# A graph network with top-p attention on one Trainium2 core: the second attention's first look moved to ScalarE, its search cut into eight steps woven over three row tiles

## The chip, the cores and the metric

The program runs on one core of a Trainium2 chip. The metric is the device time of one launch in microseconds, the median of five runs. A separate profiled execution gives the trace from which all durations below are read.

## The reference, cut to what matters

There are 3327 nodes with 256 features, a sparse weighted adjacency matrix (about 1% of the entries and the diagonal), and four layers, each followed by a residual and a normalisation over the features. The change concerns the last layer alone:

```python
def _top_p_attention(X, W1, W2, W3):
    logits = (X @ W1.T @ W2.T) @ (X @ W3.T).T
    probs = softmax(logits)                      # 3327 x 3327
    # a row keeps its largest entries until their sum reaches 0.9
    keep_sorted = cumsum(sorted) - sorted < 0.9
    A = probs * mask
    return A / A.sum(-1)
R = (S + eye) / row sums                         # S is the adjacency matrix
for n in range(2):
    A = _top_p_attention(Xa, W1, W2, W3)
    Xf = R @ Xf                                  # "diffusion"
    Xa = A @ Xa                                  # "attended values"
    Z = Z + Xf @ U1[n].T + Xa @ U2[n].T
h = layernorm(X + Z)
```

The attention is computed twice, each time over the whole graph. The second attention needs the first one's output of every row.

## The kernel before

Rows are padded to 3328 and cut into 26 row tiles of 128. A row tile of either attention passes through the following parts, which the code writes as Python generators, so that a loop can lay instructions of different tiles beside each other with `next`.

- **Logits** (`scores`, lines 698 to 709): eight matmuls of 128x416 in four pairs (line 707, tile `sc`, two PSUM buffers), each copied out by ScalarE into `e`, 128x3328 (line 708). `e` has three buffers.
- **Search** for the threshold. The first attention uses `search_short`. The second uses `search_long`, since its rows keep more entries:
  - `m8` (line 813), the largest of the first 416 logits, gives a shift; ScalarE takes exp of half of it (line 817, sum `root`) and exp (line 818, sum `tot`).
  - The first look: a guess `c1` from these sums (lines 822 to 824). ScalarE counts the entries over it with Sign (line 827) while VectorE sums them with a full-width pass (line 829, sum `m1`).
  - The second look: a better guess `c2` and its negative `nc2` (lines 830 to 846). ScalarE takes Relu (line 847) and then Sign (line 848) of the whole tile.
  - From these, `k2`, `m2` and the last guess `c3` (lines 861 to 870), 128x1 operations on VectorE in a chain. Line 873 writes `z`, the entries under `c3`, a full-width pass. Then come 26 `max` of 128 columns (line 759, `cand`), six rounds of `max` and `match_replace` over 208 candidates (lines 768 and 770), the crossing of 0.9 (lines 777 to 780), the ties (lines 881 to 892, two `match_replace` of 128x1664), and the full-width pass of line 893 that zeroes all of `e` below the threshold.
- **Attended values** (`attended`): seven groups of four 128x128 transposes on TensorE (line 747, tile `tp`), copied out by ScalarE (line 749, `wt`), and 26 matmuls of 128x256 against `G` (line 751; the trace shows two passes for each matmul).
- **Diffusion** (`diffused`, `aggregated`): 26 matmuls of 128x256 with adjacency blocks that SP's queue loads in four pieces (lines 717 and 719; three buffers), and a combination on VectorE (line 737, `xf`) with a term that GpSimd prepares (lines 728 and 732). Diffusions run up to four tiles ahead.
- **Epilogue** (`second`, lines 931 to 953): VectorE joins values and diffusion (line 934, `h`), two normalisations with statistics on VectorE (lines 83 and 84, called at each) and the power -0.5 on GpSimd (lines 507 and 508), a last scaling on ScalarE (line 950) and the store.

The loop of both attentions is one (line 984): logits of a tile, one diffusion, the three steps of the search for three neighbouring tiles, then values and epilogue. A scheduler of the language then fixes the order on each engine when the program is built, from its own costs and from the order in the source. Each engine works through its list in that order, so an instruction that waits holds up all behind it on its engine. The build can be listed engine by engine without running it.

Of the kernel before, what the change touches and what calls it, by code (L numbers as in the profile page):

```python
# [18 lines left out]
P = 128  # L19
# [9 lines left out]
DA = 64  # L29
# [4 lines left out]
RP0, RPT = 6, 6  # L34
# [3 lines left out]
DL = 4  # L38
# [4 lines left out]
def gnn_kernel(ctx: ExitStack, tc: tile.TileContext, n: int, a: dict, out: bass.AP):  # L43
# [88 lines left out]
    with tc.tile_pool(name="l1b", bufs=1) as wpool, tc.tile_pool(name="l1at", bufs=2) as l1at:  # L132
# [29 lines left out]
        with tc.tile_pool(name="l1aw", bufs=1) as cwork, tc.tile_pool(name="l1c", bufs=2) as ch, \  # L162
# [318 lines left out]
    with tc.tile_pool(name="l3", bufs=1) as pool, tc.tile_pool(name="l3d", bufs=1, space=DRAM) as dram:  # L481
# [258 lines left out]
        def attended(work, psum, e, rhs):  # L740

            acc = psum.tile([P, D], F32, name="acc")
            for j0 in range(0, nt, 4):
                m = min(4, nt - j0)
                pt = psum.tile([P, 4, P], F32, name="tp")
                for j in range(m):
                    nc.tensor.transpose(pt[:, j, :], e[:, (j0 + j) * P:(j0 + j + 1) * P], ident)  # L747
                wt = work.tile([P, 4, P], F32, name="wt", bufs=3)
                nc.scalar.copy(wt[:, :m, :], pt[:, :m, :])  # L749
                for j in range(m):  # L750
                    nc.tensor.matmul(acc, wt[:, j, :], rhs[:, j0 + j, :],  # L751
                                     start=(j0 + j == 0), stop=(j0 + j == nt - 1))
            return acc

        def segment_tops(work, z):

            cand = work.tile([P, nseg * 8], F32, name="cand")
            for s in range(nseg):
                nc.vector.max(cand[:, s * 8:(s + 1) * 8], z[:, s * SEG:(s + 1) * SEG])  # L759
            return cand  # L760

        def ranked(work, cand, rounds):

            top = work.tile([P, 8 * rounds], F32, name="top")
            rest = work.tile([P, nseg * 8], F32, name="rest", bufs=1)
            for r in range(rounds):
                left = rest if r else cand
                nc.vector.max(top[:, r * 8:(r + 1) * 8], left)  # L768
                if r + 1 < rounds:
                    nc.vector.match_replace(rest, top[:, r * 8:(r + 1) * 8], left, NEG)  # L770
            return top
# [19 lines left out]
        def search_short(work, sm, e, total, v, kept):  # L791


            top = ranked(work, segment_tops(work, e), RP0)
            neg = t1(sm, "neg")
            nc.vector.tensor_scalar_mul(neg, top[:, 0:1], -1.0)
            nc.scalar.activation(e, e, AF.Exp, bias=neg, accum_out=total)
            nc.scalar.activation(top, top, AF.Exp, bias=neg)
            crossing(work, v, top, 0.0, limit(sm, total))
            nc.vector.scalar_tensor_tensor(e, e, v, e, op0=ALU.is_ge, op1=ALU.mult, accum_out=kept)  # L800
            yield

        def search_long(work, sm, e, total, v, kept):
# [5 lines left out]
            def t(name):  # L809
                return t1(sm, name)  # L810
# [12 lines left out]
            nc.vector.tensor_mul(c1, c1, total)  # L823
            nc.vector.scalar_tensor_tensor(c1, c1, 0.301, c1, op0=ALU.mult, op1=ALU.mult)

            sg, k1, m1 = t("sg"), t("k1"), t("m1")
            nc.scalar.activation(junk, e, AF.Sign, bias=c1, scale=-1.0, accum_out=sg)  # L827
            z = work.tile([P, npad], F32, name="z", bufs=1)
            nc.vector.scalar_tensor_tensor(z, e, c1, e, op0=ALU.is_ge, op1=ALU.mult, accum_out=m1)  # L829
            nc.vector.tensor_scalar(k1, sg, -0.5, npad / 2, op0=ALU.mult, op1=ALU.add)  # L830
            rc, na = t("rc"), t("na")
            nc.vector.reciprocal(rc, c1)
            nc.vector.tensor_scalar(na, m1, lim, rc, op0=ALU.subtract, op1=ALU.mult)
# [7 lines left out]
            nc.vector.reciprocal(q, q)  # L841
            c2 = t("c2")
            nc.vector.scalar_tensor_tensor(c2, p, c1, q, op0=ALU.mult, op1=ALU.mult)

            nc2, f2, k2, m2 = t("nc2"), t("fs2"), t("k2"), t("m2")
            nc.vector.tensor_scalar_mul(nc2, c2, -1.0)
            nc.scalar.activation(junk, e, AF.Relu, bias=nc2, accum_out=f2)
            nc.scalar.activation(junk, e, AF.Sign, bias=c2, scale=-1.0, accum_out=sg)  # L848

            big = t("big")  # L850
# [22 lines left out]
            nc.vector.scalar_tensor_tensor(z, e, c3, e, op0=ALU.is_lt, op1=ALU.mult, accum_out=rest)  # L873
            nc.vector.tensor_sub(base, total, rest)
            nc.vector.scalar_tensor_tensor(base, big, 1.0, base, op0=ALU.is_lt, op1=ALU.mult)
            cand = segment_tops(work, z)
            top = ranked(work, cand, RPT)
            cs = crossing(work, v, top, base, lim)

            r, up = t("r"), t("up")  # L880
            nc.vector.tensor_sub(cs, cs, top)
# [49 lines left out]
        def second(work, psum, it, acc, f, xf):  # L931

            h = work.tile([P, D], F32, name="h")
            nc.vector.scalar_tensor_tensor(h, acc, f, xf, op0=ALU.mult, op1=ALU.add)
            yield
            xb = work.tile([P, D], F32, name="t")
            nc.gpsimd.tensor_tensor(xb, X[:, it, :], b3, op=ALU.add)
            mv = small.tile([P, 2], F32, name="mv")
            stats(mv, h)
            rs = small.tile([P, 1], F32, name="rs")  # L940
            power(rs, mv)
            nc.vector.scalar_tensor_tensor(h, h, mv[:, 0:1], g3, op0=ALU.subtract, op1=ALU.mult)
            nc.vector.scalar_tensor_tensor(h, h, rs, xb, op0=ALU.mult, op1=ALU.add)
            mv = small.tile([P, 2], F32, name="mv")
            stats(mv, h)
            rs = small.tile([P, 1], F32, name="rs")
            power(rs, mv)
            nb = small.tile([P, 1], F32, name="nb")
            nc.vector.scalar_tensor_tensor(nb, mv[:, 0:1], -1.0, rs, op0=ALU.mult, op1=ALU.mult)
            nc.scalar.activation(h, h, AF.Identity, scale=rs, bias=nb)  # L950
            m = min(P, n - it * P)
            nc.sync.dma_start(out[it * P:it * P + m, :], h[:m, :])
            yield
# [29 lines left out]
        with tc.tile_pool(name="l3w", bufs=2) as work, tc.tile_pool(name="l3s", bufs=4) as sm, \  # L983
                tc.tile_pool(name="l3at", bufs=3) as atp, tc.tile_pool(name="l3p", bufs=2, space=PSUM) as psum:


            for p, search, step, lead in ((0, search_short, first, (1,)), (1, search_long, second, (2, 1, 0))):
                es, searches, xfs, todo = {}, {}, [], None
                for i in range(-lead[0], nt):
                    t = i + lead[0]  # L990
                    parts = []
                    if t < nt:
                        q = work.tile([2 * DA, P], F32, name="q")
                        nc.sync.dma_start(q, qd[p][t])
                        es[t] = work.tile([P, npad], F32, name="e", bufs=3)
                        searches[t] = search(work, sm, es[t], *(x[p][:, t:t + 1] for x in (tots, vs, kepts)))
                        parts.append(scores(work, psum, p, q, es[t]))
                    more = range(len(xfs), min(nt, i + DL + 1))
                    for j in more[:1]:
                        parts.append(diffused(work, atp, psum, p, j, xfs))  # L1000
                    if p:
                        for x in parts:
                            both(x)
                    else:
                        both(*parts)
                    if todo is not None:
                        next(todo)
                    for part in lead:
                        if 0 <= i + part < nt:
                            next(searches[i + part])  # L1010
                    for j in more[1:]:
                        both(diffused(work, atp, psum, p, j, xfs))
                    if i >= 0:
                        tot, kept = (x[p][:, i:i + 1] for x in (tots, kepts))
                        f = normalizer(sm, kept, tot)
                        todo = step(work, psum, i, attended(work, psum, es[i], G if p else X), f, xfs[i])
                        next(todo)
                next(todo)
                fl = unresolved(sm, psum, p)
                if p == 0:  # L1020
                    fl0 = fl

            fi0 = pool.tile([1, nt + 1], I32, name="fi0")
            fi1 = pool.tile([1, nt + 1], I32, name="fi1")
            nc.vector.tensor_copy(fi0, fl0)
            nc.vector.tensor_scalar_add(fl, fl, fl0[:, nt:])
            nc.vector.tensor_copy(fi1, fl)
# [45 lines left out]
        def again(p, it):  # L1073

            with tc.tile_pool(name="l3w", bufs=2) as work, tc.tile_pool(name="l3s", bufs=1) as sm, \
# [24 lines left out]
                both((second if p else first)(work, psum, it, attended(work, psum, e, G if p else X), f, xfs[0]))  # L1100

        bad = nc.values_load(fi1[0:1, nt:nt + 1])
        with tc.If(bad > 0):
# [67 lines left out]
```

## Time and profile before

| what | value |
|---|---|
| median of five runs | 4013.08 us (4001.09 to 4016.1) |
| the profiled execution's own time | 4014.39 us |
| its span, first to last instruction | 4012.6 us |
| TensorE, VectorE, ScalarE, GpSimd busy in the span | 90%, 68%, 42%, 9% |
| mean granted TensorE clock | 0.954 |
| start of the second attention's first logits (line 707) | 3052.6 us |
| first and last start of line 873 in it | 3102.4 and 3955.7 us |

The profiled execution is 1.3 us above the median. A row of a timeline or group gives line, engine, operation, written tile, read tiles, shapes, a count where equal neighbours are merged, and in brackets the idle time before it with the instruction that ended it. "Busy" columns of a window are us in which an engine worked.

### The profile page before, as it was taken

The page shows a single profiled execution, that of the slowest core. Times are in us where ns is not written, and L with a number is a line of the kernel's source. Part 1 is how long each engine was busy: PE and PEld are TensorE (multiplying, and loading weights), DVE is VectorE, ACT ScalarE, POOL GpSimd, SP SyncE. Part 2 cuts the span into 40 slices and gives each one's busy share as a digit, 9 for nine tenths or more (in the row PEclk, how much of TensorE's full clock was granted, in tenths as well). Part 3 has the DMA queues.
Part 4 walks back from the last instruction along what each step waited for, and adds up shares of the span by engine and source line. Part 5 has one row for each costly group of instructions (what it writes and reads, how often), then busy time and mean ns, then how long its engine had stood idle before and what let it go on. Part 6 is the DMA issues. An engine that isn't in the chain of part 4 may idle for free.

```text
span 4012.6 us, 41676 instructions
## 1 busy us (share of the span) xinstructions
PE 3604.4 (90%) x15071; PEld 2626.9 (65%) x15071; DVE 2723.9 (68%) x6003; ACT 1676.1 (42%) x2690; POOL 367.8 (9%) x436
## 2 busy tenths in 40 slices
PE   8999988888888877789989999999999899999985
PEld 7888754444444433378877777777777677777764
DVE  1111579999999989867743444443452999999996
ACT  0000554555554555211112333333344666666662
POOL 0000000101010101011110000000000122222210
PEclk9999999999999988899999999999999999999997
DMA  6442211111111000044422221121103222122100
GB/s 219 138 140 92 79 47 37 37 35 35 39 34 34 23 0 0 15 146 142 140 77 79 60 57 49 53 60 52 49 25 86 59 62 58 54 60 63 55 22 7
DMA packets 98960, 252.96 MB, mean 63 GB/s; under 512 B 13858, under 2 KB 48034, under 8 KB 98610
## 3 DMA queue, kind: packets, MB, share of 16 engines
q1 hardware_dynamic: 98738, 250.14, 20.4%
q8 instruction: 122, 2.00, 0.2%
q14 instruction: 100, 0.82, 0.1%
HBM read 239.88 MB, written 10.22 MB: 62 GB/s over the span
## 4 chain that ended last, share of the span: by engine, by line
PE 34%; DVE 16%; ACT 3%; issue 2%; POOL 1%; DMA 0%; SPq 0%; POOLq 0%; ACTq 0%; DVEq 0%
PE acc L751 11%; PE acc L719 7%; PE acc L649 6%; PE sc L707 3%; DVE cand L759 3%; DVE e L892 2%; DVE e L893 2%; PE tp L747 2%; PE pj L917 1%; DVE z L829 1%; DVE top L768 1%; DVE z L873 1%; DVE rest L770 1%; ACT junk L827 1%; ACT junk L848 1%
## 5 line engine op out<-in xcount | busy, mean ns | idle before, releaser
L403 DVE TENSOR_TENSOR_SCAN h<-dA,carry,db 128x512 f32<-128x512 f32 (+1 forms) x448 | 510.4, 1189 | 0.1
L459 PE MATMUL y<-h,ident 128*128 128x512 f32 (+1 forms) x896 | 443.7, 642 | 70.6 <-DVE h L406 70.2
L759 DVE MAX8 cand<-e 128x8 f32<-128x128 f32 x676 | 143.8, 279 | 497.4 <-ACT e L708 497.4
L751 PE MATMUL acc<-G,wt 128*128 128x256 f32 x1352 | 342.9, 408 | 48.4 <-ACT wt L749 48.4
L459 PEld LDWEIGHTS y<-h,ident 128*128 128x128 f32 x896 | 188.8, 218 | 288.1 <-issue 175.7
L749 ACT COPY wt<-tp 128x512 f32<-128x512 f32 (+1 forms) x364 | 186.1, 553 | 438.2 <-PE tp L747 438.0
L751 PEld LDWEIGHTS acc<-G,wt 128*128 128x128 f32 x1352 | 268.8, 204 | 120.8 <-ACT wt L749 82.2
L234 PE MATMUL cb<-F,at 128*128 128x256 f32 x1352 | 330.6, 389 | 8.3 <-ACT m L251 8.2
L708 ACT COPY e<-sc 128x416 f32<-128x416 f32 (+1 forms) x416 | 192.6, 508 | 329.4 <-PE sc L707 329.4
L751 PE MATMUL acc<-X,wt 128*128 128x256 f32 x1352 | 326.0, 386 | 3.0 <-ACT wt L749 2.8
L719 PE MATMUL acc<-X,at 128*128 128x256 f32 x1352 | 322.2, 388 | 2.5 <-issue 2.5
L234 PEld LDWEIGHTS cb<-F,at 128*128 128x128 f32 x1352 | 259.5, 195 | 88.9 <-issue 32.8
L649 PE MATMUL acc<-F,at 128*128 128x257 f32 x1352 | 310.5, 383 | 4.0 <-DVE at L646 4.0
L719 PE MATMUL acc<-F,at 128*128 128x256 f32 x1352 | 308.8, 380 | 0.0
L113 PE MATMUL acc<-xa,at 128*128 128x257 f32 x1352 | 308.2, 381 | 0.0
L719 PEld LDWEIGHTS acc<-X,at 128*128 128x128 f32 x1352 | 251.9, 192 | 76.4 <-issue 44.6
L751 PEld LDWEIGHTS acc<-X,wt 128*128 128x128 f32 x1352 | 250.3, 191 | 63.8 <-ACT wt L749 33.5
L388 ACT ACTIVATE dA<-dt,A_log 128x512 f32<-128x512 f32 (+1 forms) x448 | 281.0, 681 | 12.5 <-DVE dt L365 12.1
L707 PE MATMUL sc<-kT,q 64*128 64x416 f32 x832 | 259.8, 561 | 27.5 <-ACT e L708 26.0
L113 PEld LDWEIGHTS acc<-xa,at 128*128 128x128 f32 x1352 | 255.6, 191 | 37.4 <-issue 0.7
L719 PEld LDWEIGHTS acc<-F,at 128*128 128x128 f32 x1352 | 249.5, 189 | 46.5 <-issue 13.7
L649 PEld LDWEIGHTS acc<-F,at 128*128 128x128 f32 x1352 | 253.6, 192 | 39.1 <-DVE at L646 4.3
(297 smaller groups left out, 5362.3 us busy)
## 6 DMA issues: line engine op xcount, KB each, us to landing
at<-in_adjT SPq DMA_DIRECT2D x104, 832.0 KB, 4.5
at<-in_adjT SPq DMA_DIRECT2D x156, 448.0 KB, 3.4
at<-in_adjT SPq DMA_DIRECT2D x52, 576.0 KB, 3.7
at<-in_adjT SPq DMA_DIRECT2D x52, 320.0 KB, 3.0
at<-in_adjT SPq DMA_DIRECT2D x26, 512.0 KB, 3.5
xa<-in_x SPq DMA_DIRECT2D x1, 3328.0 KB, 13.6
xt<-in_xT SPq DMA_DIRECT2D x26, 128.0 KB, 4.1
qd<-q SPq DMA_DIRECT2D x52, 64.0 KB, 1.5
```

The source lines that it names most:

```text
L113: nc.tensor.matmul(acc, at[:, j, :], rhs[:, j0 + j, :], start=(j0 + j == 0), stop=(j0 + j == nt - 1))
L234: nc.tensor.matmul(acc, at[:, j % JC, :], X0[:, j, :], start=(j == 0), stop=(j == nt - 1))
L388: nc.scalar.activation(dA[:, g, :], dt[:, g, :], AF.Exp, scale=A[:, g, s:s + 1])
L403: nc.vector.tensor_tensor_scan(h[:, g, :], dA[:, g, :], db[g // 2][:, g % 2, :], initial=carry[:, s, g:g + 1], op0=ALU.mult, op1=ALU.add)
L459: nc.tensor.matmul(ys[g][:, :w], ident, h[:, g, :], start=False, stop=(s == DS - 1))
L649: nc.tensor.matmul(acc, at[:, j, :], F[:, j0 + j, :], start=(j0 + j == 0), stop=(j0 + j == nt - 1))
L707: nc.tensor.matmul(pl[:, :w], q[h:h + DA, :], kT[p][h:h + DA, c0:c0 + w], start=True, stop=True)
L708: nc.scalar.copy(e[:, c:c + w], pl[:, :w])
L719: nc.tensor.matmul(acc, at[:, j, :], rhs[:, j0 + j, :], start=(j0 + j == 0), stop=(j0 + j == nt - 1))
L749: nc.scalar.copy(wt[:, :m, :], pt[:, :m, :])
L751: nc.tensor.matmul(acc, wt[:, j, :], rhs[:, j0 + j, :], start=(j0 + j == 0), stop=(j0 + j == nt - 1))
L759: nc.vector.max(cand[:, s * 8:(s + 1) * 8], z[:, s * SEG:(s + 1) * SEG])
```

## The change

Everything up to the end of the first attention is left as it was. In the second attention:

- `m1` of the first look is no longer VectorE's full-width pass: ScalarE takes Relu of `e` minus `c1` (new line 837) before the Sign (839), and VectorE computes `m1 = k1 * c1 + f1` on 128x1 (842).
- `search_long` yields seven times in place of two before its end, so it has eight steps.
- `attended` yields after each group of transposes. `second` has three steps.
- The two attentions have loops of their own. That of the second weaves eight search steps of three row tiles, the seven groups of values, half logits, and single pieces of a diffusion.
- Five diffusions are made before the second row tile's logits, and there is one iteration more, since values of a tile come one iteration after its search.

New line numbers of the parts named above: `m8` 821, exps 825 and 826, `c1` 830 to 832, `nc1` 836, Relu and Sign of the first look 837 and 839, `k1` 841, `c2` and `nc2` 855 and 857, Relu and Sign of the second look 858 and 860, `k2` 873, `z` 885, tie `match_replace` 908, last pass 909, `h` 950, second scaling 959, `nb` 966.

```diff
         def search_long(...)
...
-            sg, k1, m1 = t("sg"), t("k1"), t("m1")
+            nc1, f1, sg, k1, m1 = t("nc1"), t("fs1"), t("sg"), t("k1"), t("m1")
+            nc.vector.tensor_scalar_mul(nc1, c1, -1.0)
+            nc.scalar.activation(junk, e, AF.Relu, bias=nc1, accum_out=f1)
+            yield
             nc.scalar.activation(junk, e, AF.Sign, bias=c1, scale=-1.0, accum_out=sg)
-            z = work.tile([P, npad], F32, name="z", bufs=1)
-            nc.vector.scalar_tensor_tensor(z, e, c1, e, op0=ALU.is_ge, op1=ALU.mult, accum_out=m1)
+            yield
             nc.vector.tensor_scalar(k1, sg, -0.5, npad / 2, op0=ALU.mult, op1=ALU.add)
+            nc.vector.scalar_tensor_tensor(m1, k1, c1, f1, op0=ALU.mult, op1=ALU.add)
...
             nc.scalar.activation(junk, e, AF.Relu, bias=nc2, accum_out=f2)
+            yield
             nc.scalar.activation(junk, e, AF.Sign, bias=c2, scale=-1.0, accum_out=sg)
...
-            cand = segment_tops(work, z)
+            cand = candidates(work)
+            segment_tops(cand, z, 0, nseg // 2)
+            yield
+            segment_tops(cand, z, nseg // 2)
             top = ranked(work, cand, RPT)
             cs = crossing(work, v, top, base, lim)
+            yield
...
         def second(work, psum, it, acc, f, xf):
             h = work.tile([P, D], F32, name="h")
             nc.vector.scalar_tensor_tensor(h, acc, f, xf, op0=ALU.mult, op1=ALU.add)
-            yield
             xb = work.tile([P, D], F32, name="t")
...
             power(rs, mv)
+            yield
             nc.vector.scalar_tensor_tensor(h, h, mv[:, 0:1], g3, op0=ALU.subtract, op1=ALU.mult)
...
             power(rs, mv)
+            yield
             nb = small.tile([P, 1], F32, name="nb")
...
+            es, searches, xfs = {}, {}, []
+            for i in range(-2, nt + 1):
...
+                if 0 < i:
+                    values = attended(work, psum, es[i - 1], G)
...
+                weigh(2)
+                search(i)
+                search(i + 1)
+                weigh(2)
+                search(i + 1)
+                weigh(3)
+                search(i)
+                if 0 < i:
+                    f = normalizer(sm, kepts[1][:, i - 1:i], tots[1][:, i - 1:i])
+                    result = second(work, psum, i - 1, next(values), f, xfs[i - 1])
+                next(result, None)
+                logits = start(1, i + 2, es, searches, search_long) if i + 2 < nt else iter(())
+                more = range(len(xfs), min(nt, max(i, 0) + DL + 1))
+                spread = diffused(work, atp, psum, 1, more[0], xfs) if more else iter(())
+                next(logits, None)
+                next(logits, None)
+                next(spread, None)
+                search(i + 1)
+                both(logits)
+                next(spread, None)
+                search(i + 1)
+                search(i + 2)
+                next(result, None)
+                both(spread)
+                search(i)
+                for _ in result:
+                    pass
+                for j in more[1:]:
+                    both(diffused(work, atp, psum, 1, j, xfs))
```

More of the change, by code (lines that the diff above doesn't have):

```diff
@@ L752, in attended, with last_of, segment_tops, candidates @@
                                      start=(j0 + j == 0), stop=(j0 + j == nt - 1))
[L753 to L758, printed above, removed]
+                yield None
+            yield acc
+        def last_of(steps):
+            *_, x = steps
+            return x
+        def segment_tops(cand, z, lo=0, hi=nseg):
+            for s in range(lo, hi):
                 nc.vector.max(cand[:, s * 8:(s + 1) * 8], z[:, s * SEG:(s + 1) * SEG])
-            return cand
+        def candidates(work):
+            return work.tile([P, nseg * 8], F32, name="cand")
         def ranked(work, cand, rounds):
@@ L791, in search_short @@
         def search_short(work, sm, e, total, v, kept):
-            top = ranked(work, segment_tops(work, e), RP0)
+            cand = candidates(work)
+            segment_tops(cand, e)
+            top = ranked(work, cand, RP0)
             neg = t1(sm, "neg")
@@ L875, in search_long @@
             nc.vector.scalar_tensor_tensor(base, big, 1.0, base, op0=ALU.is_lt, op1=ALU.mult)
-            cand = segment_tops(work, z)
+            cand = candidates(work)
+            segment_tops(cand, z, 0, nseg // 2)
+            yield
+            segment_tops(cand, z, nseg // 2)
             top = ranked(work, cand, RPT)
             cs = crossing(work, v, top, base, lim)
+            yield
             r, up = t("r"), t("up")
@@ L984, in gnn_kernel @@
                 tc.tile_pool(name="l3at", bufs=3) as atp, tc.tile_pool(name="l3p", bufs=2, space=PSUM) as psum:
[L987 to L1021, printed above, removed]
@@ new lines, in start @@
+            def start(p, t, es, searches, search):
+                q = work.tile([2 * DA, P], F32, name="q")
+                nc.sync.dma_start(q, qd[p][t])
+                es[t] = work.tile([P, npad], F32, name="e", bufs=3)
+                searches[t] = search(work, sm, es[t], *(x[p][:, t:t + 1] for x in (tots, vs, kepts)))
+                return scores(work, psum, p, q, es[t])
+            es, searches, xfs, todo = {}, {}, [], None
+            for i in range(-1, nt):
+                parts = []
+                if i + 1 < nt:
+                    parts.append(start(0, i + 1, es, searches, search_short))
+                more = range(len(xfs), min(nt, i + DL + 1))
+                for j in more[:1]:
+                    parts.append(diffused(work, atp, psum, 0, j, xfs))
+                both(*parts)
+                if todo is not None:
+                    next(todo)
+                if i + 1 < nt:
+                    next(searches[i + 1])
+                for j in more[1:]:
+                    both(diffused(work, atp, psum, 0, j, xfs))
+                if i >= 0:
+                    f = normalizer(sm, kepts[0][:, i:i + 1], tots[0][:, i:i + 1])
+                    todo = first(work, psum, i, last_of(attended(work, psum, es[i], X)), f, xfs[i])
+                    next(todo)
@@ new lines, in gnn_kernel, with search, weigh @@
+            next(todo)
+            fl0 = unresolved(sm, psum, 0)
+            es, searches, xfs = {}, {}, []
+            for i in range(-2, nt + 1):
+                def search(t):
+                    if 0 <= t < nt:
+                        next(searches[t])
+                values, result = iter(()), iter(())
+                if 0 < i:
+                    values = attended(work, psum, es[i - 1], G)
+                def weigh(steps):
+                    for _ in range(steps):
+                        next(values, None)
+                weigh(2)
[25 more added lines that the diff above has]
+                    pass
+                for j in more[1:]:
+                    both(diffused(work, atp, psum, 1, j, xfs))
@@ L1023, in gnn_kernel @@
+            fl = unresolved(sm, psum, 1)
             fi0 = pool.tile([1, nt + 1], I32, name="fi0")
@@ L1099, in again @@
                 both(diffused(work, atp, psum, p, it, xfs))
-                both((second if p else first)(work, psum, it, attended(work, psum, e, G if p else X), f, xfs[0]))
+                acc = last_of(attended(work, psum, e, G if p else X))
+                both((second if p else first)(work, psum, it, acc, f, xfs[0]))
         bad = nc.values_load(fi1[0:1, nt:nt + 1])
```

## The prediction

> **What bounds it now.** I read the page's totals first, then stage windows, then single rows.
>
> ```profile
> core 0: us, PE busy (x) PEld busy (x) DVE busy (x) ACT busy (x) POOL busy (x), PEclk, DMA share, GB/s
> 3049.00:3169.70 120.70, 104.67 (x450) 79.79 (x449) 78.57 (x269) 76.43 (x79) 11.46 (x17) 0.94 0.34 95
> 3169.70:3955.70 786.00, 697.37 (x3178) 538.55 (x3178) 740.94 (x2588) 517.76 (x583) 166.17 (x177) 0.95 0.18 51
> 3955.70:4012.60 56.90, 35.71 (x158) 28.93 (x156) 29.72 (x97) 8.58 (x16) 3.80 (x8) 0.80 0.02 7
> ```
>
> These windows cut the second attention by its marker, the `z` pass (line 873), once per row tile: fill until the third marker, 23 gaps, drain. A gap is 786.0 / 23 = 34.17 us. VectorE works 32.2 us of it, TensorE 30.3, ScalarE 22.5. VectorE sets the pace; TensorE is 2 us behind.
>
> The drain shows the search of one tile alone on VectorE:
>
> ```profile
> 3955.67 3.69 DVE L873 SCALAR_TENSOR_TENSOR z<-e,c 128x3328 f32<-128x3328 f32 x1
> ...
> 3964.69 0.38 DVE L768 MAX8 top<-cand 128x8 f32<-128x208 f32 x1
> ...
> 3971.94 1.87 DVE L892 MATCH_REPLACE8 e<-drop,e 128x1664 f32<-128x1664 f32 x1
> ...
> 3975.98 3.67 DVE L893 SCALAR_TENSOR_TENSOR e<-e,v 128x3328 f32<-128x3328 f32 x1
> 3979.59 0.08 DVE L893 DVE_READ_ACCUMULATOR e<-e,v 128x1 f32 x1
> ```
>
> From marker to the end of line 893: 24.0 us, less 0.4 for an `h` in it: 23.6.
>
> The fill shows the second look with nothing beside it:
>
> ```profile
> 3071.51 0.15 DVE L846 TENSOR_SCALAR nc<-c 128x1 f32<-128x1 f32 x1
> 3071.76 3.07 ACT L847 ACTIVATE junk<-e,nc 128x3328 bf16<-128x3328 f32 x1 [2.40 <-DVE s L855]
> 3074.96 3.07 ACT L848 ACTIVATE junk<-e,c 128x3328 bf16<-128x3328 f32 x1
> 3078.15 0.15 DVE L861 TENSOR_SCALAR k<-sg 128x1 f32<-128x1 f32 x1 [3.54 <-ACT junk L848]
> 3079.80 0.22 DVE L870 SCALAR_TENSOR_TENSOR c<-c,c,big 128x1 f32<-128x1 f32 x1
> ```
>
> A ScalarE pass takes 3.20 us, start to start. `nc2` to `k2` takes 6.6 us; `k2` to the next marker 1.9. **The question is what VectorE does in those 6.6 us.** In the order of the build before, all 25 gaps have `nc2` among the first `max` instructions: the two passes lie beside 26 `max`, the ranking and the ties.
>
> **The change, part by part.**
>
> *VectorE's pass leaves.* One 3.68 us pass per tile goes; `nc1` and the new `m1` add 0.15 and 0.20 (rows of lines 846 and 862). VectorE falls to 32.2 - 3.3 = 28.9 us a gap, ScalarE rises to 22.5 + 3.2 = 25.7, TensorE stays at 30.3. If no wait took its place, TensorE would set about 31.
>
> *A longer first look.* `c1` to `k1` was one ScalarE pass beside VectorE's own; it is now two, 6.4 us. In most gaps of the new order `nc1` stands near 10 us after the marker and `k1` after the ranking (4.8) and the crossing (2.4), 17.2 or later. 10 + 6.4 = 16.4: covered, cost 0. Without that cover it would be up to 6.4.
>
> *The second look is moved.* This is the costly part. I listed the new build's VectorE order and sorted the 23 gaps by where `nc2` stands: **early**, before both tie `match_replace` (6 gaps); **middle**, between them or before the last full-width pass, line 909 (5); **late**, behind line 909 (12).
>
> Late, from marker 0: 23.6 alone, 0.4 for `xf`, 0.6 for the next tile's `c1` and `nc1`, 1.0 for `k1` and its followers: line 909 ends at 25.6. The rest of the chain to `nc2` (rows of lines 839 to 846, 0.97): 26.6. Then ScalarE's list: Relu 3.2, one `wt` of 256 columns (0.37), two `sc` copies (0.92), Sign 3.2: `k2` at 34.3. Meanwhile VectorE has only `m8` and the epilogue. In seven of the twelve, `m8` stands behind `nc2` and needs an `sc` copy that stands behind Relu, so it waits until 30.7; 0.7 for it and 3.6 for the epilogue (drain, line 934 at 3998.84 to the second line 84 ending 4002.45) give 35.0. `nb`, in the middle of the `k2` chain, waits 1.26 more for GpSimd (4002.27 to 4003.53): 36.2, and 1.3 of chain: 37.5. Four of the seven also begin with the previous epilogue's second half, +1.2: 38.7. In the five others `m8` comes before: 0.7 later at `nc2`, no `wt`, 34.6 + 1.9 = 36.5. Sum: 3 x 37.5 + 4 x 38.7 + 5 x 36.5 = 449.8. Ends: 34.9 each (no copies between the passes, epilogue hidden: 26.6 + 6.4 + 1.9) and 38.9.
>
> Middle: `nc2` near 22.0, passes and copies to 29.8, the chain mixed with the epilogue to 31.7 to 33.3; 32.6, so 163.0. Early: no VectorE wait over 1 us; TensorE's 30.3 plus 0.9, a fraction of its present 3.9 idle, as its copies still queue behind ScalarE's passes: 31.2, so 187.2. Ends for these 11: 30.5 and 34.2.
>
> Gaps: 449.8 + 163.0 + 187.2 = 800.0, against 786.0: **+14.0 us**.
>
> *The fill.* The first marker comes at about 3083 instead of 3102, since the second tile's first look no longer stands ahead of it on VectorE. But five diffusions of 11.5 us now precede the second tile's logits on TensorE: 3051 + 57.5 = 3108.6, logits 6.2 (four pairs at 1.56), two exps 6.9, `c1` 0.7, first look with three `sc` copies between 8, to `nc2` 2, second look 7, chain 1.9: second marker 3141, third 31 later, 3172. Before: 3169.7. **+2.3**; between -5 and +8.
>
> *The drain.* The last tile's search has half of an epilogue inside (0.5 + 0.8): **+1.3**.
>
> *Moved at nothing:* GpSimd's powers and memsets keep their neighbours but for the next epilogue's bias sum, which may stand ahead of a power: 0.7 (row of line 732) up to 4.2 if it meets a full-width pass, inside the `nb` wait above. SP's queue issues the same loads; `at` pieces land in 3.4 us with three buffers ahead, and a TensorE gap hides them. If not, 1 us a gap.
>
> *TensorE's clock.* After a long pause TensorE is slow:
>
> ```profile
> 3979.81 1.94 PE L747 MATMUL tp<-ident,e 128*128 128x128 f32 x8 [5.26 <-DVE e L893]
> 3981.63 5.47 PE L751 MATMUL acc<-G,wt 128*128 128x256 f32 x16
> 3986.93 1.04 PE L747 MATMUL tp<-ident,e 128*128 128x128 f32 x8
> 3988.26 3.72 PE L751 MATMUL acc<-G,wt 128*128 128x256 f32 x16 [0.15 <-ACT wt L749]
> ```
>
> That is 0.9 + 1.75 = 2.65 us lost. A late gap leaves TensorE 7 us idle, so such pauses grow, but they fit in that idle time: 0 in the sum.
>
> The Trainium skill, "TensorE: Matmul & The Clock Gate", section "What's actually happening", says that an idle window of about 3.4 us halves the clock and as long a busy one restores it. An estimate by that page: 1.7 us lost per pause, 39 us if each of 23 gaps had one on the path, which would make 4070.
>
> The Trainium skill, "ScalarE: Activation LUTs", section "Step-by-step: what each stage is for", gives one element per cycle, 0.833 ns, thus 2.77 us for 3328 columns by estimate; the row says 3.20. By the page the late gaps would be 0.86 shorter, 10 us in all, making 4020.
>
> **Sum.** 4014.4 (profiled execution) + 14.0 + 2.3 + 1.3 = 4032.0; that execution stands 1.3 above the median: **4031 us**.
>
> **The rivals.** About 0.2%, 8 us, is what can be told from no change: 4005 to 4021.
>
> - *The weave works as the source is laid out* (0.20): VectorE's small operations slip between passes, so `nc2` comes out early enough and all gaps cost a middle one: 23 x 32.6 = 749.8, 36.2 less than now: 3980. For it: VectorE's 28.9 us. Against: lists are worked in order, and `nc2` is behind line 909 in 12 of 23. It decides where 6.6 us of VectorE work lie between `nc2` and `k2`.
> - *TensorE is the new bound everywhere* (0.05): 23 x 31.2 = 717.6: 3948. It needs no late gap to wait.
> - *Both sides cancel* (0.10): late gaps at 36.4: 436.8 + 163.0 + 187.2 = 787.0: about 4017.
> - *Late gaps spoil the others* (0.17): their pauses slow TensorE, transposes and `wt` copies come late, and ScalarE's passes queue behind them; early and middle gaps stay at 34.2: 449.8 + 376.2 = 826.0: 4057.
>
> **How the numbers follow.** The forecast has 0.48. Its own unknowns (late gaps at 34.9 to 38.9) reach from 4000 to 4047. The range 3975 to 4070 leaves out the TensorE-bound case and the outer ends of the first and last rivals, 0.2 together. Faster by over 0.2%: 0.25, the first two rivals; within: 0.10, the cancelling one; slower: 0.65, the forecast and the last.
>
> **What would show it.** Right: line 829's group gone, line 837 with 26 passes near 3.07 us; VectorE's share of the gaps down from 94% to about 84%; waits of `k2` (873) for Sign (860), of `m8` (821) for line 708 and of `nb` (966) for GpSimd, together 4 to 6 us per late gap; marker gaps in two groups, near 31 to 33 and 36 to 39, in the order of the list. First marker near 3083, second near 3141. Wrong: even gaps below 33, VectorE still above 90% busy, or `k2` never waiting. A row tile flagged as unresolved by the new `m1` would show as full-width passes in the repeat code and cost over 100 us (28 passes of 3.7); I see no sign of it.

## The result, and the profile after

The changed kernel takes 4021.86 us (median of 29 runs, 4016.44 to 4036.09), the kernel before 4010.56 us in the same comparisons (54 runs). The ratio is 1.003 with a 95% interval of 1.0023 to 1.0037: 9 to 15 us slower, where 18 were forecast. The profiled execution took 4022.87 us, its span is 4021.1.

The same three stages of the second attention after the change (fill, 23 gaps between markers, drain; columns as before):

```profile
core 0: us, PE busy (x) PEld busy (x) DVE busy (x) ACT busy (x) POOL busy (x), PEclk, DMA share, GB/s
3049.00:3165.40 116.40, 102.06 (x429) 76.56 (x429) 66.79 (x261) 77.53 (x80) 15.06 (x17) 0.92 0.32 92
3165.40:3961.40 796.00, 713.53 (x3187) 541.75 (x3188) 691.79 (x2593) 591.33 (x635) 99.47 (x176) 0.95 0.18 50
3961.40:4021.10 59.70, 32.72 (x146) 26.34 (x144) 29.96 (x96) 7.64 (x15) 3.74 (x8) 0.79 0.03 9
```

VectorE's work in the 23 gaps fell from 740.9 to 691.8 us, ScalarE's rose from 517.8 to 591.3, and the stage became 10 us longer, 786 to 796. Now no engine is busy for more than 90% of it. The work that left VectorE had set the pace there, and waits took its place. The waits of VectorE between 3100 and 3970 us (who waits, for whom; us in total, times, longest):

```profile
DVE k L873 <- ACT junk L860: 27.0, 8, 6.7
DVE m L821 <- ACT e L708: 24.9, 10, 3.4
DVE nb L966 <- POOL rs L508: 20.0, 23, 1.4
DVE h L959 <- POOL rs L508: 12.4, 19, 0.8
```

Before, `k2` waited 15.7 us for ScalarE in this stretch, `m8` did not appear among the waits, and `nb` waited 18.2. (The stretch is a little longer than the 23 gaps; one wait of `k2`, 6.7 us, lies in the fill.) One late gap on VectorE, from marker 3682.6 to marker 3720.2 (37.6 us), shows how the waits hang together:

```profile
3704.74 3.68 DVE L909 SCALAR_TENSOR_TENSOR e<-e,v 128x3328 f32<-128x3328 f32 x1
...
3709.18 0.15 DVE L857 TENSOR_SCALAR nc<-c 128x1 f32<-128x1 f32 x1
...
3713.22 0.59 DVE L821 MAX8 m<-e 128x8 f32<-128x416 f32 x1 [3.43 <-ACT e L708]
...
3716.46 0.48 DVE L959 SCALAR_TENSOR_TENSOR h<-h,rs,t 128x256 f32<-128x256 f32 x1 [0.77 <-POOL rs L508]
...
3717.53 0.12 DVE L873 TENSOR_SCALAR k<-sg 128x1 f32<-128x1 f32 x1
...
3718.68 0.16 DVE L966 SCALAR_TENSOR_TENSOR nb<-mv,rs 128x1 f32<-128x1 f32 x1 [0.77 <-POOL rs L508]
...
3720.21 3.69 DVE L885 SCALAR_TENSOR_TENSOR z<-e,c 128x3328 f32<-128x3328 f32 x1
```

`nc2` comes after the full-width pass of line 909, so the tile's whole search is done before the next tile's second look begins. From `nc2` to the marker pass 11 us, in which VectorE has `m8`, the epilogue and a chain of 128x1 operations, and stands still for 3.43 us because the copy that `m8` needs is behind Relu on ScalarE:

```profile
3709.36 3.07 ACT L858 ACTIVATE junk<-e,nc 128x3328 bf16<-128x3328 f32 x1 [4.38 <-DVE nc L857]
3712.34 0.19 ACT L858 ACTIVATION_READ_ACCUMULATOR junk<-e,nc 128x1 f32 x1
3712.43 0.35 ACT L749 COPY wt<-tp 128x256 f32<-128x256 f32 x1
3712.68 0.91 ACT L708 COPY e<-sc 128x416 f32<-128x416 f32 x2
3713.48 3.09 ACT L860 ACTIVATE junk<-e,c 128x3328 bf16<-128x3328 f32 x1
```

The drain's first transposes and values, to be set beside those of before (5.26 us pause, then 1.94 and 5.47):

```profile
3986.76 1.94 PE L747 MATMUL tp<-ident,e 128*128 128x128 f32 x8 [10.20 <-DVE e L909]
3989.46 0.25 PE L988 MATMUL pj<-f,ones 128*1 128x26 f32 x2 [0.77 <-DVE f L986]
3989.64 5.96 PE L751 MATMUL acc<-G,wt 128*128 128x256 f32 x16
```

### The profile page after: what moved, and what is told of

It is laid out like the page before. It is cut to its first block, busy times and chain, and to the rows that moved or that the text cites. A ratio compares the mean times of both kernels' runs of the same rounds, so it can differ in the third digit from the quotient of the medians.

```text
span 4021.1 us, 41701 instructions
## 1 busy us (share of the span) xinstructions
PE 3609.6 (90%) x15071; PEld 2625.1 (65%) x15071; DVE 2663.1 (66%) x6003; ACT 1749.5 (44%) x2742; POOL 306.6 (8%) x436
## 4 chain that ended last, share of the span: by engine, by line
PE 34%; DVE 16%; issue 3%; ACT 3%; POOL 1%; DMA 1%; SPq 0%; POOLq 0%; ACTq 0%; DVEq 0%
PE acc L719 9%; PE acc L751 9%; PE acc L649 6%; PE sc L707 4%; DVE cand L763 3%; DVE e L908 2%; DVE top L774 2%; DVE rest L776 2%; PE tp L747 2%; DVE e L909 1%; PE pj L933 1%; DVE z L885 1%; ACT e L708 1%; POOL rs L508 1%; PE pj L938 1%
## 5 line engine op out<-in xcount | busy, mean ns | idle before, releaser
L719 PE MATMUL acc<-F,at 128*128 128x256 f32 x1352 | 332.0, 396 | 0.0
L719 PEld LDWEIGHTS acc<-F,at 128*128 128x128 f32 x1352 | 257.5, 197 | 66.5 <-issue 26.5
L707 PE MATMUL sc<-kT,q 64*128 64x416 f32 x832 | 264.6, 572 | 38.4 <-ACT e L708 36.8
L113 PEld LDWEIGHTS acc<-xa,at 128*128 128x128 f32 x1352 | 255.3, 190 | 37.3 <-issue 0.7
L649 PEld LDWEIGHTS acc<-F,at 128*128 128x128 f32 x1352 | 254.8, 193 | 37.3 <-DVE at L646 2.4
```

The lines of the kernel that those rows point to most:

```text
L113: nc.tensor.matmul(acc, at[:, j, :], rhs[:, j0 + j, :], start=(j0 + j == 0), stop=(j0 + j == nt - 1))
L649: nc.tensor.matmul(acc, at[:, j, :], F[:, j0 + j, :], start=(j0 + j == 0), stop=(j0 + j == nt - 1))
L707: nc.tensor.matmul(pl[:, :w], q[h:h + DA, :], kT[p][h:h + DA, c0:c0 + w], start=True, stop=True)
L719: nc.tensor.matmul(acc, at[:, j, :], rhs[:, j0 + j, :], start=(j0 + j == 0), stop=(j0 + j == nt - 1))
```

## The experiments

The prediction's reason was the place of `nc2`: late gaps are long, early ones short. The first four experiments took the change apart and put `nc2` where it was wanted; "gap" is the distance between markers in each kernel's own trace, and "23 gaps" run from the third marker to the last; waits are those within the 23 gaps. The gaps are what can be compared best: in the traces of kernels with the same first attention, the second attention begins anywhere between 3042.7 and 3058.0 us.

**`nc2` early in every gap.** Before the tie `match_replace`, which is the first long piece that a late `nc2` stands behind, the value is made to depend on the next tile's `nc2`.

```diff
+            after = v
+            if it + 1 in nc2s:
+                after = t("after")
+                nc.vector.scalar_tensor_tensor(after, nc2s[it + 1], 0.0, v, op0=ALU.mult, op1=ALU.add)
...
-                nc.vector.tensor_scalar_add(drop, drop, v)
+                nc.vector.tensor_scalar_add(drop, drop, after)
```

> The changed kernel, with one 128x1 operation per row tile that makes the two tie match_replace of a tile wait for nc2 of the next tile (nc2 times 0, added to the threshold: no value changes). The build's VectorE order then has nc2 ahead of both match_replace in all 23 gaps, in place of 6. Theory (the place of nc2 sets the gap): the 12 late and 5 middle gaps of 37.6 and 32.6 us fall to early ones, which measured 30.4 in the changed kernel; in this order nc1 stands later, behind one or two rounds of the ranking, so k1 may wait 1 to 2 us for the Sign: 30.4 to 32.5 each, 23 gaps 699 to 748 in place of 796, so 48 to 97 us less than the changed kernel, 3925 to 3974 us. Rival (the long gaps come from ScalarE's queue, which has one pass more, or from TensorE, and nc2 is late as a result): the gaps stay at 34.6 on average, time within 10 us of the changed kernel.

Measured: 4016.96 us, ratio 1.0018 (1.0005 to 1.0031). The 23 gaps take 788.4 us, 34.3 each: 7.6 less than in the changed kernel, nothing like the gain expected. `k2` hardly waits any more (3.8 us), but `k1` of the first look now does (46.6 us, in 20 of the 23 gaps; in the changed kernel it waited for nothing there). The gaps alternate: 37.7, 32.0, 37.3, 32.8, 37.7, 32.0 and so on. The place of `nc2` alone does not decide.

**`nc2` late in every gap.** The last VectorE operation ahead of `c2` is made to depend on the sum of the previous tile's last pass.

```diff
+            if it - 1 in ends:
+                nc.vector.scalar_tensor_tensor(q, ends[it - 1], 0.0, q, op0=ALU.mult, op1=ALU.add)
             nc.vector.scalar_tensor_tensor(c2, p, c1, q, op0=ALU.mult, op1=ALU.mult)
```

> The mirror of the first: nc2 of a tile is made to wait for the sum of the previous tile's last full-width pass, and that step is called ahead of it, so nc2 is late in all 23 gaps. Between nc2 and k2 the order leaves VectorE only nb. Theory: each gap about 37.5 to 39: 23 gaps 863 to 897 in place of 796, so 67 to 101 us more than the changed kernel, 4088 to 4123 us. Rival (ScalarE's or TensorE's load sets the gap): within 15 us of the changed kernel.

Measured: 4086.53 us, ratio 1.0196 (1.0173 to 1.0218). The gaps are 35.8 to 37.5 and `k2` waits 114.1 us for Sign, once in each. The time is 1.5 us under the low end of what was expected, the price of a late gap, 36.9 in the mean, a little under the 37.5 forecast. Late is dear, as said; early is not cheap by itself.

**The weave alone**: the changed kernel with the first look's sum back on VectorE.

```diff
-            nc1, f1, sg, k1, m1 = t("nc1"), t("fs1"), t("sg"), t("k1"), t("m1")
-            nc.vector.tensor_scalar_mul(nc1, c1, -1.0)
-            nc.scalar.activation(junk, e, AF.Relu, bias=nc1, accum_out=f1)
+            sg, k1, m1 = t("sg"), t("k1"), t("m1")
+            z = work.tile([P, npad], F32, name="z", bufs=1)
+            nc.vector.scalar_tensor_tensor(z, e, c1, e, op0=ALU.is_ge, op1=ALU.mult, accum_out=m1)
...
-            nc.vector.scalar_tensor_tensor(m1, k1, c1, f1, op0=ALU.mult, op1=ALU.add)
```

> The changed kernel with the first look as it was before: Sign on ScalarE beside a full-width pass on VectorE; the loop, the eight steps and the three-step epilogue stay. The build's order has nc2 early in all 23 gaps. Theory: no gap waits for the second look, VectorE is the bound again with its 32.2 us of work and 1 to 2 us of waits: gaps 33.2 to 34.2, 764 to 787, so 10 to 32 us less than the changed kernel, 3990 to 4012, equal to or a little under the kernel before. Rival (the weave itself costs: fill, drain, three-step epilogue, queued copies): slower than the kernel before by 10 us or more.

Measured: 4009.65 us, ratio 1.0005 (0.9993 to 1.0016). The gaps are 31.9 to 37.9 us long, 781.5 us for 23: no gain and no loss in the time.

**The look alone**: the kernel before with the converse of that edit, in its old loop.

> The kernel before with only the first look moved to ScalarE; loop, three search steps and two-step epilogue as before. The build's order has nc2 late in 13 gaps, middle in 1, early in 9. Theory: 13 x 37.5 + 32.6 + 9 x 30.4 = 794 against 786 us, so about 8 us more than the kernel before, 4010 to 4030: the move of the look alone brings the late order and its loss. Rival (the move of the look helps and the weave takes it back): VectorE's 3.3 us per gap are gained, 3935 to 3960.

Measured: 4028.99 us, ratio 1.0047 (1.0028 to 1.0066); `nc2` is late in 13 gaps. `m8` waits 27.5 us, `k2` 20.1 and `nb` 36.8. That the time lies in the expected range is in part luck: the late gaps take 39.3 us, not 37.5, so that the 23 gaps take 818.1 us and not 794, and a fill that is 17.5 us shorter than before (99.6 us from the first logits to the third marker, against 117.1) hides most of it. Still, it is the moved look, not the weave, that costs the time.

Apart from the all-late kernel, the mean gaps of these and of the kernel before lie between 34.0 and 35.6, however `nc2` is placed. That suggested a common bound behind the placements: the three `e` buffers, since a buffer is held for about three gaps. The next four experiments tested that theory. A fourth buffer only fits if the first attention's tables are released, so a control came with it, in which the repeat code is left out too.

```diff
+        passing = ExitStack()
+        kp = passing.enter_context(tc.tile_pool(name="l3k", bufs=1))
...
+        passing.close()
+        with tc.tile_pool(name="l3w", bufs=2) as work, tc.tile_pool(name="l3s", bufs=4) as sm, \
...
-                es[t] = work.tile([P, npad], F32, name="e", bufs=3)
+                es[t] = work.tile([P, npad], F32, name="e", bufs=4 if p else 3)
```

> Control for the next two. The changed kernel with U1, U2 and the first attention's key table in a pool that is closed when the first attention is done, work pools of its own for the second attention, and the repeat code for flagged rows left out (it is not entered with these inputs). The second attention's lists are the same, 12 late, 5 middle and 6 early gaps. All theories: as the changed kernel, 4022 within 10 us, 23 gaps of 34.6 us in the mean.

Measured (control): 4030.69 us, ratio 1.0051 (1.0035 to 1.0066), 23 gaps in 794.4 us. The gaps are those of the changed kernel, and from its first logits to the end the second attention takes 973.0 us in the trace, as there (973.1). What makes the control slower, 8.8 us by the medians, lies ahead of the second attention; that it is the price of the released tables is not shown, since that beginning scatters by more between the traces.

> The control with four e buffers in place of three in the second attention (room for a fourth is what the control makes). The next tile's logits may then be copied before the last tile's transposes have read the oldest buffer. The listed order becomes 1 late, 16 middle and 6 early gaps. Theory A, the life of an e buffer (logits, exps, two looks, the marker pass to the last pass, transposes, about three gaps) sets the pace of every kernel so far: the gaps fall to 31 to 32.6 us, 40 to 80 us less than the control, 3945 to 3980. Theory B, ScalarE's serial list with its four round trips per tile, or TensorE's 31.0 busy us per gap, sets it: gaps stay above 34, the time within 12 us of the control.

Measured: 4007.09 us, ratio 0.9992 (0.9981 to 1.0004): 24 us under the control, less than either bound of the buffer theory and more than its rival allowed. The gaps settle at 34.1, nearly all alike, with no engine busy for more than 31.2 us of one.

> Four e buffers and nc2 held early in all 23 gaps by making the tie match_replace of the tile before depend on it. With three buffers the same gate moved the wait from k2 to k1 and won 5 us. Theory A: with the fourth buffer the logits, exps and first look come a gap earlier, k1 waits for nothing, gaps of 31 to 32 us, TensorE as the bound: 3940 to 3965. Theory B: k1 waits as before, 53 us in all, and the time stays at 4005 to 4020.

Measured: 4047.14 us, ratio 1.0092 (1.0074 to 1.0111): both theories missed. Gaps of 35.2 and 36.9, 807.7 us for 23, slower than with three buffers.

> The new weave with the first look back on VectorE, now with four e buffers; nc2 is early in 23 gaps. VectorE works 32.4 us per gap. Theory A: the gaps fall from 34.0 to about 32.8, VectorE becomes the bound, 20 to 35 us less than with three buffers: 3975 to 3992, and slower than the versions with the look on ScalarE and four buffers, which is where the moved look would at last bring something. Theory B: 4009 within 10 us.

Measured: 4023.21 us, ratio 1.0034 (1.0022 to 1.0046), 23 gaps in 790.2 us where three buffers took 781.5 (and 970.5 against 959.4 from the first logits to the end, which leaves the control's later beginning out): both theories missed again. The buffer theory fell: a fourth buffer helped in one order and harmed in two.

What set those even gaps could be read in their traces. With `nc2` early and three buffers, one gap of 32.9 us (markers 3536.5 and 3569.4) on ScalarE and TensorE:

```profile
3549.33 3.07 ACT L839 ACTIVATE junk<-e,nc 128x3328 bf16<-128x3328 f32 x1 [1.69 <-DVE rc L846]
3552.30 0.19 ACT L839 ACTIVATION_READ_ACCUMULATOR junk<-e,nc 128x1 f32 x1
3552.39 1.05 ACT L749 COPY wt<-tp 128x512 f32<-128x512 f32 x2
```

```profile
3547.87 1.04 PE L747 MATMUL tp<-ident,e 128*128 128x128 f32 x8
3548.83 0.97 PE L707 MATMUL sc<-kT,q 64*128 64x416 f32 x4
3553.01 6.65 PE L751 MATMUL acc<-G,wt 128*128 128x256 f32 x16 [3.21 <-ACT wt L749]
...
3572.78 1.02 PE L751 MATMUL acc<-G,wt 128*128 128x256 f32 x4
```

The transposes are done at 3548.9, but in ScalarE's list the first look's Relu stands ahead of their `wt` copies. TensorE idles 3.21 us and then takes 6.65 us for sixteen passes that take 3.72 at full clock. The values end at 3573.8, in the next gap, whose epilogue starts late: that gap is the one of 37.7 us. In the tile after it the list has the copies ahead of Relu, and no such pause. (So the expectation below, which gives the length of 37 us to the gaps that hold the pause, has it one gap off: they are 32.0 to 32.9 themselves, and the following ones are long.) With four buffers and early `nc2`, 19 of 23 gaps had Relu ahead of the copies, and with four buffers alone 18. With the look on VectorE, where Sign is the pass in question, it was 12 gaps with four buffers and 3 with three.

In the changed kernel itself the copies stand ahead of Relu in all 23 gaps, but `nc2` is early in only 6. The new theory: **both** are needed. The last three experiments held Relu behind two copies:

```diff
+                lastwt[:] = [wt[:, m - 1, P - 1:]] if rhs is G else []
...
-            nc.vector.tensor_scalar_mul(nc1, c1, -1.0)
+            if lastwt:
+                zero = t("zero")
+                nc.scalar.activation(zero, lastwt[0], AF.Identity, scale=0.0)
+                nc.scalar.activation(nc1, c1, AF.Identity, scale=-1.0, bias=zero)
+            else:
+                nc.vector.tensor_scalar_mul(nc1, c1, -1.0)
             nc.scalar.activation(junk, e, AF.Relu, bias=nc1, accum_out=f1)
```

> Three e buffers, nc2 held early as in the first experiment, and the first look's Relu held behind the first two wt copies: its negative guess nc1 is made on ScalarE and takes a zero from the last column of the second wt tile (two 128x1 operations on ScalarE more, one on VectorE less). ScalarE's list then has the two wt copies ahead of Relu and Sign of the first look in every gap; without the hold it alternated. Theory A, ScalarE's list between the transposes and their copies sets the gap: in the first experiment the gaps that began with Relu ahead of the copies (TensorE idle 3.2 us at 3553.0, its next sixteen passes 6.65 in place of 3.72) took 37.3 to 37.7, those with the copies ahead 32.0 to 32.9. All gaps would then be of the short kind, about 32.7 with the two small operations: 23 x 32.7 = 752 in place of 788, 3980 plus or minus 12, faster than both kernels. Theory B, a long gap follows a short one whatever the order, since a loop over two tiles (an e buffer's life of three gaps, or the epilogue) has to be made up: the mean stays at 34.3 and the time at 4010 to 4025.

Measured: **3977.47 us, ratio 0.9917 (0.99 to 0.9933)**, faster than both kernels. From the seventh marker to the fourth last the gaps are 32.4 to 32.7. Its windows (the 23 gaps) and one gap's TensorE rows:

```profile
3173.90:3917.20 743.30, 700.59 (x3204) 536.76 (x3203) 688.59 (x2594) 611.56 (x684) 91.14 (x178) 0.98 0.19 55
```

```profile
3569.05 1.03 PE L749 MATMUL tp<-ident,e 128*128 128x128 f32 x8
3570.02 0.96 PE L707 MATMUL sc<-kT,q 64*128 64x416 f32 x2
3570.91 3.72 PE L754 MATMUL acc<-G,wt 128*128 128x256 f32 x16
```

The pause is gone, sixteen passes take 3.72 us, and TensorE is busy for 94% of the stage (700.6 of 743.3), where the changed kernel had 90%. The waits of `k1` fall from 46.6 to 21.1 us. VectorE's work is that of the changed kernel (688.6 against 691.8).

> Four e buffers, nc2 held early, and the first look's Relu held behind two wt copies as in the run before. With four buffers and without the hold all gaps had Relu ahead of the copies and took 35.2 to 36.9. Theory A: 32 to 33 us a gap, 23 x 32.5 = 748 in place of 808 us, time 3980 to 3995. Theory B: gaps stay at 35 to 37, 4035 to 4055.

Measured: 3967.28 us, ratio 0.9895 (0.9877 to 0.9912), the fastest of all and 13 us better than the low end expected. The gaps are 32.2. The hold alone turned 4047 into 3967. Without it, this kernel shows the price of the pause and of the slow clock apart. In 17 gaps ScalarE's list around the pause is the same, and so is the pause (2.78 to 2.81 us); in ten of them TensorE's clock fell and the sixteen passes took 5.41 us, in seven it stayed at 1.00 and they took 3.72:

```profile
3599.92 3.72 PE L753 MATMUL acc<-G,wt 128*128 128x256 f32 x16 [2.78 <-ACT wt L751]
...
3635.11 5.41 PE L753 MATMUL acc<-G,wt 128*128 128x256 f32 x16 [2.80 <-ACT wt L751]
```

The gap that follows takes 36.9 us after each of the ten and 35.2 after six of the seven (36.0 after the last). So of the 4.7 us between 36.9 and the 32.2 with the hold, 1.7 are the clock, and the other 3.0 are about the length of the pause. The hold also moves later copies: in these gaps the third pair stood behind both passes of the second look, with the hold it stands between them. What the first pair is worth by itself was not measured.

> The changed kernel with the first look's Relu held behind two wt copies and nothing else; nc2 stays where the listed order has it: 12 late, 8 middle, 3 early gaps. Theory A by itself says the early and middle gaps get short, while the late gaps stay long through k2's wait: 12 x 37.5 + 11 x 32 = 802 us, 4015 to 4030, no gain without the early nc2. Theory B: the same range. A time under 4000 would say that the place of nc2 does not matter at all.

Measured: 4021.88 us, ratio 1.003 (1.0019 to 1.0041), as the changed kernel. Without the early `nc2` the hold is worth nothing.

Together, in mean gaps of three-buffer kernels (each 23 gaps divided by 23):

| `nc2` | ScalarE's list as it came | Relu held behind two copies |
|---|---|---|
| where the order put it | 34.6 (the change) | 34.6 |
| early | 34.3 | 32.3 |

The weave with the look on VectorE has `nc2` early in all 23 gaps and the copies ahead of its Sign in 20, and its gaps are 34.0, of which VectorE is busy for 32.3. So the moved look is worth about 1.7 us a gap (34.0 against 32.3), once both conditions hold; the hold with the look on VectorE was not tried.

## Why the prediction was right, and where it was off

*VectorE's pass leaves.* The added ScalarE pass took 3.07 us, 26 times, as forecast, and ScalarE's share is the 25.7 us a gap that was named. VectorE fell by 2.1 us a gap (32.2 to 30.1), not by 3.3, to 87% instead of 84%. The durations of its single records did fall by 3.5 us a gap, 81.6 in all; but fewer of them overlap in time, 148 us in the 23 gaps against 177 before.

*The longer first look is covered.* Right: `k1` waited 6.4 and 6.7 us, both in the fill, and for nothing in the gaps.

*The moved second look.* Right, and not only in the sum. Late gaps: 451.0 us for the 12, forecast 449.8, and they fall into the three kinds that were worked out: 38.7 us in the mean for the four that begin with half an epilogue (forecast 38.7), 37.9 for the three others with `m8` behind `nc2` (37.5), 36.5 for the five with `m8` ahead of it (36.5). Middle: 162.7, forecast 163.0. In the 12 late gaps the waits of `k2`, `m8` and `nb` come to 15.6, 24.1 and 14.7 us, 4.5 per gap, within the 4 to 6 named. **The early gaps were mis-sized**: 182.3 us for 6, or 30.4 each, where 31.2 was taken. This is the largest error of the sum, 4.9 us. The 23 gaps took 10.0 us more than before; 14.0 were forecast.

*The fill.* In this execution the second attention began 4.65 us earlier than in the one before (3047.98 against 3052.63). Put on the clock of before, the first three markers come at 3083.2, 3139.5 and 3170.1; forecast 3083, 3141 and 3172. The fill costs 0.4 us, not 2.3.

*The drain.* 2.8 us, not 1.3. The search part is 1.2 longer (25.2 against 24.0), which was foreseen; the rest was not. TensorE has paused 10.2 us, and the first `wt` copy waits at the end of ScalarE's list for the epilogue's scaling `h` (3988.50) before it starts at 3989.00, though its four transposes were done.

The sum of the second attention is then 10.0 + 0.4 + 2.8 = 13.2 us in the traces, where the timed ratio gives 12 and the forecast was 17.6. The errors of the terms go both ways (early gaps and fill too dear, late gaps and drain too cheap), so the nearness of the sum owes something to luck. Of the 9 us between 4031 and 4021.86, 2.5 lie in the starting value: the kernel before has a median of 4010.56 us in 54 runs, where the forecast started from 4013.08 in five.

*The rivals.* That the late gaps spoil the others was wrong: early and middle gaps kept their own prices. That the weave works as laid out was wrong too, for the reason given against it. But the step in it that names the decision, 6.6 us of VectorE work between `nc2` and `k2`, is incomplete: with `nc2` early in all gaps the time still did not fall to the rival's 3980, because the order on ScalarE then came between TensorE's transposes and their copies. With that mended the time was 3977. The prediction priced ScalarE's passes as a delay for VectorE; for TensorE, whose copies "queue behind ScalarE's passes", it took 0.9 us in an early gap, a fraction of the idle time. Where the list had Relu ahead of the copies, TensorE paused for 2.3 to 3.2 us, and lost 1.7 to 3.0 more where its clock fell.

*TensorE's clock.* The prediction put pauses at nothing. In the changed kernel few decide anything: of 58 timeline rows of sixteen passes in the 23 gaps 6 took longer than 4.5 us, 10.7 us over 3.72 each in all. With early `nc2` and no hold it was 12 of 68 rows, with the hold 3 of 68. So the slow clock is a part of what the hold saved with three buffers, not the whole: of the 45.1 us by which the 23 gaps became shorter, 11.9 are busy time of TensorE (712.5 to 700.6) and 33.2 idle time (75.9 to 42.7).

*The price of a ScalarE pass.* The prediction set 2.77 us, an estimate by the page "ScalarE: Activation LUTs" of the Trainium skill (section "Step-by-step: what each stage is for"), against the row's 3.20 start to start. The new passes of lines 837 and 839 start 3.19 us apart in the fill (3061.73 and 3064.92), so the row held: a pass is 3.07 us long and 0.19 us go to reading its sum, where the estimate counted the elements alone. That the time came near the page's 4020 is the doing of the early gaps, the fill and the starting value, not of shorter passes.

## What to carry to other kernels

When an engine is relieved of work by giving it to an engine that also serves a third, ask not only whether the receiver has room, but what stands behind the new work in its list: in the kernel with early `nc2` a 3 us pass on ScalarE, idle a quarter of the time, held TensorE's copies. A wait that is forced away at one place tells little until the trace shows which wait is next: with three buffers, only removing both made the kernel faster than the one before. And a regular pattern of gaps in which no engine is full can be a closed loop through several in-order lists: follow one period of it along the chain of waits, and look there for the order to change. What sets the even 34.1 us with four buffers alone was not settled.

## What the runs showed of the hardware

A pause of about 3 us can be enough to halve TensorE's clock. In the run with early `nc2` and three buffers the granted clock was 1.00 just before the pause of 3.21 us and 0.50 after it (windows of that run):

```profile
3547.00:3549.80 2.80, 2.80 (x17) 1.80 (x15) 2.77 (x17) 1.11 (x3) 0.00 (x0) 1.00 0.75 189
3553.00:3555.00 2.00, 1.99 (x5) 1.64 (x6) 1.84 (x12) 2.00 (x2) 0.00 (x0) 0.50 0.24 68
3555.00:3557.00 2.00, 2.00 (x6) 1.57 (x5) 0.61 (x7) 1.50 (x2) 0.00 (x0) 0.50 0.00 0
```

All ten pauses of 3.18 to 3.26 us in the gaps of that run were followed by a clock of 0.50. With four buffers and early `nc2` it was 10 of 17 pauses of 2.78 to 2.81 us; after one of 2.78 us the sixteen passes took 5.41 us, at a mean clock of 0.78 and then 0.61. With four buffers alone it was 2 of 17 pauses of 2.33 to 2.37 us, and in the kernel before a pause of 1.98 us (at 3650.71) was followed by 0.50 too. So pauses of one length are followed by either clock, and the runs give no shortest pause. The Trainium skill, "TensorE: Matmul & The Clock Gate", section "What's actually happening", says that the clock falls after an idle window of about 3.4 us. All these pauses were shorter, so here the measurement decides. The loss per pause that slowed the clock was 2.93 us (6.65 - 3.72) in the first case shown and 1.69 (5.41 - 3.72) with four buffers; the prediction's estimate by that page was 1.7.
